# Cross-attention in a decoder block: keys and values of four heads as 11 block products in place of 12

## The chip, the cores and the metric

The kernel runs on one core of a Trainium2 chip. A core has five engines that run their own instruction queues and meet at semaphores: TensorE (PE in the profile, its weight loads PEld), VectorE (DVE), ScalarE (ACT), GpSimd (POOL) and SyncE (SP), whose queue issues the transfers. The metric is the time of one execution on the device in microseconds (us).

## The reference, cut to what matters

A decoder block over x (8 batches of 224 rows of 512) with three sublayers: self-attention with soft-clamped scores, cross-attention to a context (8 batches of 750 rows of 384), and a feed-forward layer with ternary weights. Each is followed by a layer norm of the sum with its input. The change concerns the cross-attention:

```python
q = split_heads(x @ Wq)            # 16 heads of 64
k = split_heads(context @ Wk)      # Wk, Wv: 384 x 1024
v = split_heads(context @ Wv)
sim = jnp.einsum('bhid,bhjd->bhij', q, k) * SCALE
attn = jax.nn.softmax(sim, axis=-1)
out = jnp.einsum('bhij,bhjd->bhid', attn, v)
out = out.transpose(0, 2, 1, 3).reshape(b, sq, HEADS * DIM_HEAD)
return out @ Wo + bo
```

Everything in this sublayer is float32.

## The kernel before

The kernel has three stages, each with an order of work written out by hand (`manual_schedule`): on every engine the instructions stand in the order in which the program writes them, and an engine waits when the next one's operands or buffers are not ready.

Self-attention runs 32 turns (`for m in range(NS)`), each for a pair of heads and two batches. In it GpSimd computes one inverse square root per turn (L129, `nm_i`). Weights lie in a pool of four equal buffers (tag `w`): `wq`, `wk`, `wv`, then `attn_Wo`. When the first three are free, near the end of the stage, `xattn_Wk`, `xattn_Wq` and `xattn_Wv` take their places.

Cross-attention runs over 64 units, one for each batch `b` and pair of heads `hp`, in the loop `for n in range(-1, len(units))`. Turn n does, in TensorE's order:

- `scores` of unit n (L785): six blocks of 125 keys, two heads each. ScalarE copies each block to `cpT` (L793), VectorE takes maxima over the blocks (L795, L799).
- `weighted` of unit n−1 (L879), values times exponentials.
- `keys` of unit n+1 (L748), in two halves of 375 context rows: three products of 128x128 weights with 128x375 context each (384 = 3 x 128). ScalarE copies each half to `ckT` (L755).
- `queries` of unit n+1 (L761). VectorE scales them to `cqT` (L769).
- `half_values` (L736): half the rows of the values for four heads, three row tiles of 125 by 256 columns, three products each; ScalarE copies to `cv` (L743).

Meanwhile VectorE brings the maxima across partitions (`across`: L813 reduces both the maxima and the sums `csm` of the unit before), writes them to `mx_b` (L849) and adds them to the scores (L859), ScalarE exponentiates (L867), and GpSimd adds the exponentials of the six blocks (L869 to L871) into `csm`. `normalise` (L892, L896) scales the weighted sums of unit n−1. The context of a batch lies in one tile `cT`, loaded again for each batch.

Beside this a generator, `weight_steps`, prepares the feed-forward weights, one step per turn: ScalarE sums magnitudes (L643, 12 steps), then rounds (L666) and stores (L676), VectorE clamps (L669). When a batch's last pair is done, `cross_finish` projects its rows (L194) and adds them (L905 on GpSimd, L906).

The pool of PSUM banks (`ps_mm`) has seven that go round: every tile waits for the readers of the one seven before it. A float32 matmul of the program stands in the trace as two records.

Of the kernel before, what the change touches and what calls it, by code (L numbers as in the profile page):

```python
# [10 lines left out]


# [1 line left out]

# [20 lines left out]
SC, CD = 750, 384  # L35
# [11 lines left out]
CT = 125  # L47
NCT = SC // CT
HALF = SC // 2
QH = 4  # L50
NCHUNK = 4
CHUNK = DIM * HID // P // NCHUNK
# [10 lines left out]
def decoder_block(ctx: ExitStack, tc: tile.TileContext, a: dict, out: bass.AP):  # L63
# [47 lines left out]
    wq, wk, wv = ws  # L111
    for i in range(NX // 2, NX):
        load_x(i)
    wo = load_w("attn_Wo", INNER // P, DIM)

    ident = const.tile([P, P], F32, name="ident")
    make_identity(nc, ident)
# [99 lines left out]
    with tc.tile_pool(name="a_sb", bufs=2) as sb, tc.tile_pool(  # L217
# [215 lines left out]
        def self_output(g, i, hp0=0, hp1=NPAIR):  # L433
# [21 lines left out]
            nc.vector.tensor_tensor(x[i], mm, x[i], ALU.add)  # L455
            due.append(i)

        tails, outs, due, scales = {}, {}, [], []

        for i in range(4):  # L460
# [32 lines left out]
        for m in range(NS):  # L493
            g, hp = divmod(m, NPAIR)
            if m > 0:
                self_values(m - 1)
            self_scores(m)
            for i in due:
                scales.append(layernorm([i]))
            due.clear()  # L500
            if m + 1 < NS:
                scale_qk(m + 1)
            if m + 2 < NS:
                project_qk(m + 2)
            sums = inverse_sums(m)
            next(sums)
            if m + 2 < NS:
                head_norms(m + 2)

            c = 1 - hp // 4  # L510
            tiles = opened[g + hp // 4] if g + hp // 4 < NG else ()
            if hp % 4 < len(tiles):
                project_v(tiles[hp % 4], c)
            for _ in sums:
                pass
            for f in scales:
                f()
            scales.clear()
            ahead = opened[g + 1] if g + 1 < NG else ()
            if 2 <= hp < 2 + len(ahead):  # L520
                transpose_xn(ahead[hp - 2])
                copy_xn(ahead[hp - 2])
            if hp in out_at[g]:
                self_output(g - 1, closed[g - 1][out_at[g].index(hp)])
            if hp == 0:
                for i in ahead:
                    square(i)
                if ahead:
                    rms_norms(ahead[0], ahead[-1] + 1)
            if 1 <= hp < 1 + len(ahead):  # L530
                scale_x(ahead[hp - 1])
            if m == NS - 3:
                xwk = load_w("xattn_Wk", KC, INNER)
                xwq = load_w("xattn_Wq", KD, INNER)
                xwv = load_w("xattn_Wv", KC, INNER)

        last = closed[NG - 1]
        for i in last[:2]:
# [12 lines left out]
    wmean = const.tile([P, 3], F32, name="wmean")  # L551
    wscale = const.tile([P, 3], F32, name="wscale")
    parts = const.tile([P, 3, NCHUNK], F32, name="w_parts")
    dram = ctx.enter_context(tc.tile_pool(name="dram", bufs=1, space=bass.MemoryType.DRAM))
    ternary = [dram.tile([P, NCHUNK, CHUNK], BF16, name=f"tern{i}") for i in range(3)]

    wdeq = const.tile([P, 3], F32, name="wdeq")
# [50 lines left out]
    with tc.tile_pool(name="c_sb", bufs=2, reuse_waits="tile") as sb, tc.tile_pool(  # L608
# [1 line left out]
    ) as ps_mm, tc.tile_pool(  # L610
        name="c_ov", bufs=1, space=PSUM, reuse_waits="tile"
    ) as ps_ov, tc.manual_schedule(engines=ENGINES):
        def load_context(b):
            cT = sb.tile([P, KC, SC], F32, name="cT", bufs=1)
            nc.sync.dma_start(
                out=cT, in_=a["ctxT"][b].rearrange("(k p) s -> p k s", p=P)
            )
            return cT

        cT = load_context(0)  # L620
        xwo = load_w("xattn_Wo", INNER // P, DIM)
        bo = sb.tile([P, DIM], F32, name="bo", bufs=1)
        nc.sync.dma_start(out=bo, in_=a["xattn_bo"].partition_broadcast(P))
        stage = sb.tile([P, 2, CHUNK], F32, name="w_stage", bufs=1)
# [64 lines left out]
        def weight_steps():  # L689

            chunks = [(i, c) for i in range(3) for c in range(NCHUNK)]
            stage_chunk(*chunks[0], 0)
            for n, (i, c) in enumerate(chunks):
                yield
                if n + 1 < len(chunks):
                    stage_chunk(*chunks[n + 1], (n + 1) % 2)
                weight_sum(i, c, n % 2)
            yield
            stage_chunk(*chunks[0], 0)
            weight_means()  # L700
            before = None
            for n, (i, c) in enumerate(chunks):
                for h in range(CHUNK // PIECE):
                    yield
                    if before:
                        weight_store(*before)
                    if h == 0 and n + 1 < len(chunks):
                        stage_chunk(*chunks[n + 1], (n + 1) % 2)
                    before = (i, c, n % 2, h)
                    late.append(weight_round(*before))  # L710
            yield
            weight_store(*before)

# [12 lines left out]

        VN = QH * DH

        def values(cT, g, v, half):

            for c0, n in ((3 * half, 2), (3 * half + 2, 1)):
                mm = ps_mm.tile([CT, 2, VN], F32, tag="mm", name="mm_v")
                for i in range(n):
                    c = c0 + i
                    for k in range(KC):
                        nc.tensor.matmul(  # L736
                            mm[:, i, :],
                            lhsT=cT[:, k, c * CT : (c + 1) * CT],
                            rhs=xwv[:, k, g * VN : (g + 1) * VN],
                            start=(k == 0),  # L740
                            stop=(k == KC - 1),
                        )
                nc.scalar.copy(v[:, c0 : c0 + n, :], mm[:, 0:n, :])  # L743

        def keys(cT, hp, kT, c):
            mm = ps_mm.tile([P, HALF], F32, tag="mm", name="mm_k")
            for k in range(KC):
                nc.tensor.matmul(  # L748
                    mm,
                    lhsT=xwk[:, k, hp * P : (hp + 1) * P],  # L750
                    rhs=cT[:, k, c * HALF : (c + 1) * HALF],
                    start=(k == 0),
                    stop=(k == KC - 1),
                )
            nc.scalar.copy(kT[:, c * HALF : (c + 1) * HALF], mm)  # L755

        def queries(xT, hp):
            qT = sb.tile([P, S], F32, name="cqT")
            mm = ps_mm.tile([P, S], F32, tag="mm", name="mm_q")
            for k in range(KD):  # L760
                nc.tensor.matmul(  # L761
                    mm,
                    lhsT=xwq[:, k, hp * P : (hp + 1) * P],
                    rhs=xT[:, k, :],
                    start=(k == 0),
                    stop=(k == KD - 1),
                )

            nc.vector.tensor_scalar(qT, mm, SCALE, None, ALU.mult)  # L769
            return qT  # L770

        def scores(kT, qT):
# [153 lines left out]
        units = [(b, hp) for b in range(B) for hp in range(NPAIR)]  # L926
        steps = weight_steps()
        kq, vs, outs = {}, {}, {}
        late = []

        def half_values(n):

            g = (n + 1) // 2
            if g < len(units) // 2:
                if (n + 1) % 2 == 0:
                    vs[g] = sb.tile([CT, NCT, VN], F32, name="cv")
                values(cT, g % (NPAIR // 2), vs[g], (n + 1) % 2)

        END_U = len(units) - 1
        for n in range(-1, len(units)):  # L940
            if n >= 0:
                b, hp = units[n]
                pT = scores(*kq.pop(n))
                res = across(n == 0, False)
                nm = negated_maxima(res)
                norm = norm_at.get(n)
                if norm is None or norm[0] is not roots:
                    next(steps, None)
            if n >= 1:
                ov = weighted(units[n - 1][1], got, vs[(n - 1) // 2])  # L950
            if n < END_U:
                nb, nhp = units[n + 1]
                if nhp == 0:
                    transpose_x(nb)
                kT = sb.tile([P, SC], F32, name="ckT")
                keys(cT, nhp, kT, 0)
            if n >= 0:
                exponentials(pT, nm)
                got = pT
            if n < END_U:  # L960
                keys(cT, nhp, kT, 1)
                kq[n + 1] = (kT, queries(xT[nb], nhp))
            if n >= 1:
                normalise(*units[n - 1], ov, res)
            if n < END_U:
                half_values(n)
                if nhp == NPAIR - 1 and nb + 1 < B:
                    cT = load_context(nb + 1)
            for f in late:
                f()  # L970
            late.clear()
            if n >= 0 and norm is not None:
                norm[0](*norm[1:])
            if n >= 1 and units[n - 1][1] == NPAIR - 1:

                for i in completes[units[n - 1][0]]:
                    if i != NX - 3:
                        cross_finish(i)
            if n == END_U - 1:
                wg = load_ternary(0, KD, HID)  # L980
                wu = load_ternary(1, KD, HID)
                wd = load_ternary(2, HID // P, DIM)
# [230 lines left out]
```

## Time and profile before

| | |
|---|---|
| Time, median of 3 runs | 1693.07 us (1692.1 to 1693.45) |
| The profiled execution | 1693.18 us, span 1691.4 us |
| TensorE busy, share of the span | 1674.4 us, 99% |
| LDWEIGHTS | 1076.8 us, 64% |
| VectorE | 1247.2 us, 74% |
| ScalarE | 879.1 us, 52% |
| GpSimd | 628.9 us, 37% |
| Keys, L748 | 768 records, 258.5 us busy |
| Values, L736 | 1152 records, 259.1 us busy |
| Granted TensorE clock | 0.999 |

The span is the profiled execution from its first to its last instruction. Busy time of a group is the time in which at least one of its instructions ran: matmuls overlap, so the mean of one (485 ns for keys) is longer than the distance of its start from the next. In the timeline a row has the start, the length and the count of instructions that follow each other; a bracket tells how long the engine was idle before and what ended that. "waits" gives, for an engine's line, the microseconds in all, the times and the longest.

### The profile page before, as it was taken

To read this page: it belongs to the slowest core of one execution; us is meant where nothing else is said; L and a number is where in the kernel's file an instruction comes from. 1 tells how busy PE (TensorE), PEld (TensorE's weight loads), DVE (VectorE), ACT (ScalarE), POOL (GpSimd) and SP (SyncE) were. 2 spreads that over 40 slices of the span, in tenths; PEclk is the share of its full clock that TensorE was granted. 3 is DMA by queue.
4 is the path that set the end of the run, shared out by engine and by line. 5 is a ranking of instruction groups with operands and counts; after the bars stand their busy time and mean duration, and the time that the engine had idled before them with its cause. 6 is when DMAs were issued, how large, how long until landed. Compare 5 with 4: busy or idle time off the path is not lost.

```text
span 1691.4 us, 23310 instructions
## 1 busy us (share of the span) xinstructions
PE 1674.4 (99%) x8602; PEld 1076.8 (64%) x8602; DVE 1247.2 (74%) x2776; ACT 879.1 (52%) x1492; POOL 628.9 (37%) x507
## 2 busy tenths in 40 slices
PE   8999999999999999999999999999999999999998
PEld 4555554555546777776776776776776776774443
DVE  3777776767865776776886886897875776886877
ACT  4655544545523664654664664563453544445663
POOL 3333332333411443443443443443443443443244
PEclk9999999999999999999999999999999999999999
DMA  8000000000133222211221121110000000031333
GB/s 286 1 1 1 1 1 1 1 1 1 38 115 109 76 99 75 75 35 38 69 72 38 54 87 38 36 43 7 1 29 3 4 28 1 1 150 30 71 83 105
DMA packets 61956, 80.47 MB, mean 48 GB/s; under 512 B 36753, under 2 KB 38801, under 8 KB 59409
## 3 DMA queue, kind: packets, MB, share of 16 engines
q1 hardware_dynamic: 61840, 78.97, 14.5%
q8 instruction: 68, 1.11, 0.3%
q14 instruction: 48, 0.39, 0.1%
HBM read 60.34 MB, written 9.96 MB: 42 GB/s over the span
## 4 chain that ended last, share of the span: by engine, by line
PE 97%; DVE 1%; DMA 1%; issue 0%; SPq 0%; POOL 0%; POOLq 0%; DVEq 0%
PE mm_k L748 15%; PE mm_v L736 15%; PE mm_qk L279 12%; PE sc_c L785 9%; PE ov_c L879 9%; PE mm_o L446 6%; PE mm_q L761 6%; PE mm_co L194 6%; PE mm_v L325 6%; PE mm_f L1014 5%; PE sc_a L348 3%; PE ov_a L418 3%; PE dn L1102 2%; DMA cT<-ctxT 1%; PE tr_x L254 0%; PE tr_x L719 0%
## 5 line engine op out<-in xcount | busy, mean ns | idle before, releaser
L869 POOL TENSOR_TENSOR csh<-cpT 125x672 f32<-125x672 f32 x128 | 207.4, 1621 | 577.8 <-DVE cpT L859 552.0
L867 ACT ACTIVATE cpT<-cpT 125x1344 f32<-125x1344 f32 x128 | 169.6, 1325 | 228.9 <-DVE cpT L859 220.1
L748 PE MATMUL mm_k<-cT,xattn_Wk 128*128 128x375 f32 x768 | 258.5, 485 | 1.2 <-DMA cT<-ctxT 1.1
L736 PE MATMUL mm_v<-xattn_Wv,cT 128*125 128x256 f32 x1152 | 259.1, 379 | 0.0
L129 POOL TENSOR_TENSOR nm_i<-nm_q,mhalf 128x28 f32<-128x28 f32 x32 | 153.2, 4786 | 271.1 <-DVE nm_q L306 262.5
L736 PEld LDWEIGHTS mm_v<-xattn_Wv,cT 128*125 128x125 f32 x1152 | 216.3, 188 | 28.9
L793 ACT COPY cpT<-sc_c 125x448 f32<-125x448 f32 x384 | 173.7, 561 | 104.2 <-PE sc_c L785 104.1
L748 PEld LDWEIGHTS mm_k<-cT,xattn_Wk 128*128 128x128 f32 x768 | 140.0, 189 | 101.0 <-issue 12.2
L859 DVE TENSOR_TENSOR cpT<-cpT,mx_b 125x1344 f32<-125x1344 f32 x128 | 193.2, 1550 | 2.2
L795 DVE TENSOR_TENSOR cm<-sc_c,cpT 125x448 f32<-125x448 f32 x128 | 73.9, 619 | 146.5 <-ACT cpT L793 146.5
L785 PE MATMUL sc_c<-cqT,ckT 64*125 64x224 f32 x1536 | 163.1, 358 | 0.0
L879 PE MATMUL ov_c<-cpT,cv 125*64 125x224 f32 x1536 | 159.4, 357 | 0.0
L785 PEld LDWEIGHTS sc_c<-cqT,ckT 64*125 64x125 f32 x1536 | 140.3, 184 | 24.7 <-ACT ckT L755 15.0
L879 PEld LDWEIGHTS ov_c<-cpT,cv 125*64 125x64 f32 x1536 | 104.6, 137 | 47.3 <-issue 18.2
L755 ACT COPY ckT<-mm_k 128x375 f32<-128x375 f32 x128 | 59.2, 462 | 126.1 <-PE mm_k L748 126.1
L358 ACT ACTIVATE pr<-sc_a 128x448 f32<-128x448 f32 (+1 forms) x128 | 61.8, 536 | 91.2 <-PE sc_a L348 91.1
L279 PE MATMUL mm_qk<-xnT,wq 128*128 128x448 f32 (+2 forms) x280 | 107.0, 527 | 1.5 <-DVE xnT L258 1.4
L761 PE MATMUL mm_q<-xT,xattn_Wq 128*128 128x224 f32 x512 | 107.1, 352 | 0.0
L761 PEld LDWEIGHTS mm_q<-xT,xattn_Wq 128*128 128x128 f32 x512 | 96.7, 189 | 16.3
L279 PE MATMUL mm_qk<-xnT,wk 128*128 128x448 f32 x256 | 101.5, 539 | 0.0
L325 PE MATMUL mm_v<-wv,xnT 128*128 128x512 f32 x224 | 100.4, 592 | 0.0
L1014 PE MATMUL mm_f<-ternary,xqT 128*128 128x512 bf16 x448 | 98.7, 379 | 0.9 <-DVE x L906 0.9
(131 smaller groups left out, 2530.2 us busy)
## 6 DMA issues: line engine op xcount, KB each, us to landing
cT<-ctxT SPq DMA_DIRECT2D x8, 1125.0 KB, 5.3
w_stage<-w_gateT SPq DMA_DIRECT2D x8, 1024.0 KB, 4.9
w_stage<-w_upT SPq DMA_DIRECT2D x8, 1024.0 KB, 5.1
w_stage<-w_downT SPq DMA_DIRECT2D x8, 1024.0 KB, 5.2
tern<-w_t SPq DMA_DIRECT2D x24, 256.0 KB, 2.0
ternary<-tern SPq DMA_DIRECT2D x3, 2048.0 KB, 12.4
x<-x SPq DMA_DIRECT2D x14, 256.0 KB, 7.4
out<-x SPq DMA_DIRECT2D x14, 256.0 KB, 2.3
```

Of the source, the lines that this page charges most:

```text
L279: nc.tensor.matmul(mm[:, c0:c1], lhsT=(wq, wk)[w][:, k, hp * P : (hp + 1) * P], rhs=xnT[:, k, g % 2 * G + c0 : g % 2 * G + c1], start=(k = ...
L325: nc.tensor.matmul(mm, lhsT=xnT[:, k, at : at + P], rhs=wv[:, k, c * 512 : (c + 1) * 512], start=(k == 0), stop=(k == KD - 1),)
L736: nc.tensor.matmul(mm[:, i, :], lhsT=cT[:, k, c * CT : (c + 1) * CT], rhs=xwv[:, k, g * VN : (g + 1) * VN], start=(k == 0), stop=(k == KC ...
L748: nc.tensor.matmul(mm, lhsT=xwk[:, k, hp * P : (hp + 1) * P], rhs=cT[:, k, c * HALF : (c + 1) * HALF], start=(k == 0), stop=(k == KC - 1),)
L761: nc.tensor.matmul(mm, lhsT=xwq[:, k, hp * P : (hp + 1) * P], rhs=xT[:, k, :], start=(k == 0), stop=(k == KD - 1),)
L785: nc.tensor.matmul(sc[j][:, i, :], lhsT=kT[h0 : h0 + DH, ct * CT : (ct + 1) * CT], rhs=qT[h0 : h0 + DH, :], start=True, stop=True,)
L793: nc.scalar.copy(pT[:, j, 2 * c2 : 2 * c2 + 2, :], sc[j])
L859: nc.vector.tensor_tensor(pT[:, j], pT[:, j], nm[:CT, j] .rearrange("p (o q) -> p o q", o=1) .to_broadcast([CT, NCT, S]), ALU.add,)
L867: nc.scalar.activation(pT[:, j], pT[:, j], AF.Exp)
L869: nc.gpsimd.tensor_tensor(half, pT[:, j, 0:3], pT[:, j, 3:6], ALU.add)
L879: nc.tensor.matmul(ov[h0 : h0 + DH, :], lhsT=v[:, ct, hq * DH : (hq + 1) * DH], rhs=pT[:, j, ct, :], start=(ct == 0), stop=(ct == NCT - 1),)
L1014: nc.tensor.matmul(mm, lhsT=xqTs[i][:, k, :], rhs=w[:, k, cols], start=(k == 0), stop=(k == KD - 1),)
```

## The change

Take the context of a batch as 2 x 3 blocks A11 … A23 (two halves of 375 rows, three parts of 128 of the inner dimension) and the weights of four heads as 3 x 2 blocks B11 … B32 (128 columns each). The product has four blocks C11 … C22, each a sum of three block products: 12. The kernel after uses a bilinear scheme that needs 11, four of which have sums of blocks as operands:

- GpSimd builds the weight sums once, in the turns 0, 1, 3 and 4 of self-attention (`room_sums`), in a weight buffer that `attn_Wo` takes later (`load_wo`), and they go to DRAM (`sums_w`). Four context sums per batch are built during the batch before (`sum_context`).
- `half_products` runs the products of one operand, keys or values, for four heads. Three PSUM tiles x_, z_ and w_ accumulate; x_ is copied several times on the way, since it holds partial sums that several blocks share. ScalarE makes six copies, GpSimd adds two results (C11, C22), VectorE one (C21).
- Turns with odd n make the keys of the next two units, turns with even n the values of both units (`turn_products`); before, each turn made the keys of one and half the values. Seven products come before the queries, four after. `ckT` and `cv` have one buffer each.
- A key product streams 375 columns as before; a value product is three matmuls of 128 columns, where before one had 256.
- `xattn_Wk` and `xattn_Wv` are no longer held whole: each set of blocks is loaded at the end of a turn for the turn after next (`load_blocks`, three transfers), into `xw`.
- There are two context tiles, one for even and one for odd batches, each loaded a batch ahead.
- The queries' scaling goes from VectorE to ScalarE. Weight sums and rounds on ScalarE come after the first seven products (`acts`). No weight step is made in turns with hp = 6, in which `transpose_x` of the next batch now stands. `cross_finish` is called once per turn at most (`spare`).

```diff
+    def room_sums(j):
+        blk = room[:, : KC * INNER].rearrange("p (k g c n) -> p k c g n", k=KC, c=2, n=P)
...
+        sub = lambda y, p, q: nc.gpsimd.tensor_tensor(y, p, q, ALU.subtract)
+        sub(o1, b(0, 1), b(0, 0))
+        yield
+        sub(b(0, 1), b(1, 1), b(0, 1))
...
+            nc.sync.dma_start(out=sums_w[:, j, :, i, :], in_=y)
...
+        def load_blocks(j, g):
+            src = a[("xattn_Wk", "xattn_Wv")[j]].rearrange("(k p) n -> p k n", p=P)
+            c = 2 * g * P
+            nc.sync.dma_start(out=xw[:, j, 0:KC], in_=src[:, :, c : c + P])
+            nc.sync.dma_start(
+                out=xw[:, j, KC : KC + 2], in_=src[:, 1:KC, c + P : c + 2 * P]
+            )
+            nc.sync.dma_start(out=xw[:, j, KC + 2 :], in_=sums_w[:, j, g])
...
+            for _ in range({0: 2, 1: 3, 3: 2, 4: 3}.get(m, 0)):
+                next(room_steps[m // 3])
+            if m == 1:
+                room_load(1)
+            if m == 4:
+                load_wo()
...
-                weight_sum(i, c, n % 2)
+                acts.append(partial(weight_sum, i, c, n % 2))
...
-        def values(cT, g, v, half):
-        def keys(cT, hp, kT, c):
+        def half_products(b, j, product, dest):
...
+            x_, z_, w_ = acc
+            product(x_, a11, b11, True)
+            nc.scalar.copy(m1, x_)
+            product(z_, a12, b21, True)
+            product(z_, a13, b31, False)
+            nc.scalar.copy(c11, z_)
+            product(x_, s2, t2, False)
+            nc.scalar.copy(u2, x_)
+            product(w_, s3, t3, True)
+            product(w_, a23, b32, False)
+            nc.scalar.copy(c22, w_)
+            product(x_, s1, t1, False)
+            nc.scalar.copy(u4, x_)
+            nc.gpsimd.tensor_tensor(c11, c11, m1, ALU.add)
+            nc.gpsimd.tensor_tensor(c22, c22, u4, ALU.add)
+            yield
+            product(w_, a22, t4n, False)
+            product(w_, a23, dif, False)
+            nc.vector.tensor_tensor(c21, w_, u2, ALU.add)
+            product(x_, s4, b22, False)
+            product(x_, a13, b32, False)
+            nc.scalar.copy(c12, x_)
+            yield
...
+        def key_product(mm, c, w, start):
+            nc.tensor.matmul(
+                mm, lhsT=w, rhs=c, start=start, stop=True, skip_group_check=True
+            )
+
+        def value_product(mm, c, w, start):
+            for t in range(NCT // 2):
+                nc.tensor.matmul(
+                    mm[:, t, :], lhsT=c[:, t * CT : (t + 1) * CT], rhs=w,
+                    start=start and t == 0, stop=True, skip_group_check=True,
+                )
...
-            nc.vector.tensor_scalar(qT, mm, SCALE, None, ALU.mult)
+            nc.scalar.activation(qT, mm, AF.Identity, scale=SCALE)
...
-                pT = scores(*kq.pop(n))
+                pT = scores(kq.pop(n), qTs.pop(n))
...
+            products = turn_products(n)
+            next(products, None)
+            for f in acts:
+                f()
...
+                qTs[n + 1] = queries(xT[nb], nhp)
             if n >= 0:
                 exponentials(pT, nm)
...
+                if hp == NPAIR - 2 and b + 1 < B:
+                    transpose_x(b + 1)
+            for _ in products:
+                pass
             if n >= 1:
                 normalise(*units[n - 1], ov, res)
...
+                    load_blocks((n + 1) % 2, d % (NPAIR // 2))
+            if n >= 0:
+                if hp == NPAIR - 2 and b + 2 < B:
+                    load_context(b + 2)
+                if 2 <= hp < 6 and b + 1 < B:
+                    sum_context(b + 1, hp - 2)
...
+            if spare:
+                cross_finish(spare.pop(0))
```

## The prediction

> **What bounds the kernel now.** I read the page's busy table first, then the waits of TensorE, then the timeline of one turn engine by engine. The busy table and the waits of TensorE (who waited for whom, total us, times, longest):
>
> ```profile
> PE 1674.4 (99%) x8602; PEld 1076.8 (64%) x8602; DVE 1247.2 (74%) x2776; ACT 879.1 (52%) x1492; POOL 628.9 (37%) x507
> ...
> PE mm_k L748 <- DMA cT<-ctxT: 1.1, 2, 0.9
> ```
>
> TensorE never rests; in cross-attention it waits only 1.1 us, for a context transfer. A busy PE alone proves little, so the timeline of one turn (start us, length us, instructions) has to show that the instructions stand end to end:
>
> ```profile
> 613.30 2.54 PE L785 MATMUL sc_c<-cqT,ckT 64*125 64x224 f32 x24
> 615.76 2.49 PE L879 MATMUL ov_c<-cpT,cv 125*64 125x224 f32 x24
> 618.19 4.05 PE L748 MATMUL mm_k<-cT,xattn_Wk 128*128 128x375 f32 x12
> 622.08 1.67 PE L761 MATMUL mm_q<-xT,xattn_Wq 128*128 128x224 f32 x8
> 623.59 4.05 PE L736 MATMUL mm_v<-xattn_Wv,cT 128*125 128x256 f32 x18
> 627.56 2.54 PE L785 MATMUL sc_c<-cqT,ckT 64*125 64x224 f32 x24
> ```
>
> By differences of starts: scores 2.46, weighted sums 2.43, keys 3.89, queries 1.51, values 3.97; a turn is 14.26 us without a gap. [...] Within the runs the key records start 0.315 us apart (once 0.42, where the shape changes from the weighted sums), the value records 0.216. So every record removed shortens the turn, until another engine's loop is longer. Those engines in the same turn (ScalarE, VectorE, GpSimd):
>
> ```profile
> 614.41 2.71 ACT L793 COPY cpT<-sc_c 125x448 f32<-125x448 f32 x6 [0.48 <-PE sc_c L785]
> 616.95 1.97 ACT L643 ACTIVATE w_stage<-w_stage 128x2048 f32<-128x2048 f32 x1
> ...
> 620.38 0.47 ACT L755 COPY ckT<-mm_k 128x375 f32<-128x375 f32 x1 [1.37 <-PE mm_k L748]
> 624.29 2.79 ACT L867 ACTIVATE cpT<-cpT 125x1344 f32<-125x1344 f32 x2 [3.44 <-DVE cpT L859]
> ```
>
> ```profile
> 619.32 0.60 DVE L813 TRANSPOSE_TENSOR_REDUCE mx_r<-csm 128x14 f32<-128x448 f32 x1
> ...
> 622.64 3.02 DVE L859 TENSOR_TENSOR cpT<-cpT,mx_b 125x1344 f32<-125x1344 f32 x2
> 625.57 0.38 DVE L769 TENSOR_SCALAR cqT<-mm_q 128x224 f32<-128x224 f32 x1
> ```
>
> ```profile
> 625.75 1.62 POOL L869 TENSOR_TENSOR csh<-cpT 125x672 f32<-125x672 f32 x1 [7.97 <-DVE cpT L859]
> 627.45 0.66 POOL L870 TENSOR_TENSOR csm<-csh 125x224 f32<-125x224 f32 x1
> ...
> 631.37 0.67 POOL L871 TENSOR_TENSOR csm<-csm,csh 125x224 f32<-125x224 f32 x1
> ```
>
> There is a loop through these: VectorE reduces csm (619.32), adds the maxima (622.64), ScalarE exponentiates (624.29), GpSimd sums from 625.75 to 632.04, and the next reduction, at 619.32 + 14.26 = 633.58, needs that. The loop itself takes 632.04 − 619.32 = 12.72 us: 1.5 us of slack now.
>
> [...] eight records with 128 columns loaded and 128 streamed, from the timeline of the start:
>
> ```profile
> 14.26 1.06 PE L279 MATMUL mm_qk<-xnT,wq 128*128 128x128 f32 x8
> ```
>
> One of them lasts 0.275 (mean by shape in that window), so they start (1.06 − 0.275) / 7 = 0.112 us apart: loads do hide. [...] L870 takes 0.66 mostly, but 0.99 in the 24 turns in which it meets VectorE's rounding L669.
>
> **The change part by part.**
>
> *Keys* (removed): 12 products per batch and four heads become 11, so 24 records become 22: 2 × 0.315 = 0.63 us, in 8 × 4 = 32 groups: **−20.2**.
>
> *Values*: 36 records of 256 columns, 36 × 0.216 = 7.77 us, become 11 products × 3 tiles × 2 = 66 records of 128 columns. Price of one: 0.109 at least (the transposes L254 start so far apart[...]), 0.112 by the row above. If loads did not hide it would be the 0.188 of the LDWEIGHTS row. I take 0.110[...]: 7.26 us, 0.51 less, × 32: **−16.4** (−12 at 0.112, −18.5 at 0.109).
>
> *Context*: two alternating context tiles, loaded nine turns ahead: the 1.1 us goes: **−1.1**.
>
> *Products in one turn*: keys of two pairs in odd turns, values of both in even ones. A keys turn is 2.46 + 2.43 + 7.1 + 1.51 = 13.5 us, a values turn 13.7. Shape changes per turn stay as many. Counting from a turn's start (t = 0), the products begin at 4.9; seven end near 9.4, queries near 10.9, the last four at 13.5.
>
> *Accumulators*: x_ is copied and then accumulated further, so TensorE now waits for ScalarE. The first copy of x_ can start at 5.8 and ends at 6.25; its next product comes at 6.9. Each later copy has two products (1.26 us) before its bank is written: slack about 0.6 us. Queued behind such a wait is all of TensorE. Bounds: 0 if ScalarE is free (sc_c copies end at 3.8), 0.5 us a turn if not. I take 0.
>
> *ScalarE*: six copies per turn, 0.35 apart back to back (L755 626.98 to L743 627.33), for two key and two value copies, and the query scaling: some +1.3 us. In turns with weight preparation its work is 2.7 + 2.8 + 2.6 + 0.4 + 2.5 = 11 of 13.6. It moves: the weight sum (2.2) now stands after the seventh product's copy, 10.0 to 12.2; the query scaling and the first exponential follow at 12.5 instead of 11.0. Late next: the second exponential (15.0), the last copy c12 (15.4, or 1.9 into the next turn), the first sc_c copy by 0.8. VectorE's adds start at 10.1 then, still ahead of ScalarE, so this doesn't grow. c12 is for the later pair; the scores at t = 13.5 need c11 and c21.
>
> *VectorE*: c21 = one add of 375 columns, about 0.5, behind the maxima adds (end 12.3): ready at 12.8, scores at 13.5. The query scaling (0.38) leaves. Free of charge, hidden behind the last two products; without that cover 0.5 a keys turn, 16 in all.
>
> *GpSimd*: two adds of 375 columns per turn. Between the rows of 224 (0.66) and 512 columns (L905, 1.27): 1.0 each. c11 can run at 7.6, c22 at 10.1 to 11.1, before the exponential sums at 12.5. Context sums, 4 per batch, follow the sums. Busy 6.3 + 2.0 + 0.5 of 13.6: free.
>
> *Self-attention*: ten weight sums of 128x512 on GpSimd, 1.27 each, two or three per turn after nm_i (4.8 of a 13 us turn), and ten stores of them. The room tile's load takes the place of attn_Wo's, issued at 26.6, landed by 37; the first sum comes near 57. attn_Wo is needed from the ninth turn, near 158. Free; uncovered 12.7.
>
> *Transfers*: three loads per block set, 0.13 to 0.33 MB (0.25 MB takes 2.0 us), issued more than a turn before use, behind weight staging on SP's queue. Free. The ternary loads now wait for the last value product: up to 4 us later, but they landed 15 us before the first mm_f. One output projection per turn is the same work. [...]
>
> Sum: −20.2 − 16.4 − 1.1 + 1 = −36.7. The profiled execution took 1693.18 with a span of 1691.4, 0.1 above the median of 1693.07. So the span becomes 1654.7 and the time **1657** (1656.4 rounded up for waits at the edges).
>
> **Rivals.**
>
> *Half the gain is given back by ScalarE* (faster, less so). For: its work is moved into the dense end of the turn, and the scores' second pair reuses a bank that c12 must free. Against: by the above, the lateness is bounded by 0.8. Price: 0.5 us in the 37 turns with weight work, 18 us: 1675.
>
> *Short records don't hide their loads* (the change doesn't do what it says). Values break even at 7.77 / 66 = 0.118 and the whole change at (7.77 + 0.63) / 66 = 0.127 us. At 0.120 it is 1657 + 2112 × 0.010 = 1678. Against: the eight records at 0.112.
>
> *GpSimd's loop becomes the bound* (slower). If c11 and c22 come to stand in the loop, because late copies put them between exponential and sums[...], the loop is 12.72 + 2.0 = 14.7 us: 64 × 0.45 = +29: 1722. It decides from 1.54 us in the loop (14.26 − 12.72). For: GpSimd's slack shrinks to 0.9. Against: the copies come 1.4 us before the exponential ends.
>
> **How the numbers follow.** Forecast (1650 to 1665) 0.73; half the gain 0.13; loads not hidden 0.05, a fifth of it slower; GpSimd's loop 0.06, all but a little slower; anything else 0.03. 0.2% is 3.4 us, about what a measurement can tell from no change. Faster 0.91, same 0.02, slower 0.07. The range 1650 to 1678 takes in the lower bound of the value records (−2), fewer edges, and the half gain.
>
> **What would show it.** 704 key records 0.315 and 2112 value records 0.110 apart; turns of 13.5 and 13.7; no PE wait for DMA cT. Wrong if TensorE shows waits for the copies of x_ or for c21, a GpSimd busy without pause, or value records over 0.118 apart.

## The result, and the profile after

The changed kernel takes 1665.58 us (median of 4, 1665.15 to 1666.01) against 1693.12 for the kernel before on the same chip (1692.1 to 1693.45): ratio 0.9838, 95% interval 0.9821 to 0.9855, 27.5 us faster. The forecast was 1657: the sign holds and so does the wide range (1650 to 1678), but the time lies 0.6 us above the narrow one (1650 to 1665), and the point is 8.6 us too low.

The busy table and the head of the chain that ended last, from the page of after (engine, busy us, share, instructions; the chain's shares of the span):

```profile
span 1663.4 us, 26236 instructions
PE 1644.7 (99%) x9498; PEld 1086.4 (65%) x9498; DVE 1304.3 (78%) x2776; ACT 965.8 (58%) x1684; POOL 812.0 (49%) x677
...
PE 87%; DVE 8%; issue 2%; ACT 2%; POOL 0%; DMA 0%; POOLq 0%; SPq 0%; ACTq 0%; DVEq 0%
```

TensorE is still 99% busy, but the chain is not TensorE's alone any more: 8% of it runs through VectorE. The busy share couldn't have told this. The waits of TensorE in cross-attention (who waited for whom, total us, times, longest), from after:

```profile
PE sc_c L918 <- DVE cpT L992: 3.1, 6, 1.3
PE sc_c L918 <- DVE ckT L866: 0.4, 1, 0.4
```

The wait for the context transfer is gone. A new one has come: the scores wait for VectorE's adds of the negated maxima (L992). The listed 3.1 us are only a part of it. The timeline of TensorE shows a turn of keys and one of values without trouble, then two turns with it (start us, length us, instructions, the idle time ahead of them):

```profile
567.84 2.54 PE L918 MATMUL sc_c<-cqT,ckT 64*125 64x224 f32 x24
570.30 2.49 PE L1012 MATMUL ov_c<-cpT,cv 125*64 125x224 f32 x24
...
581.37 2.54 PE L918 MATMUL sc_c<-cqT,ckT 64*125 64x224 f32 x24
...
608.71 1.40 PE L918 MATMUL sc_c<-cqT,ckT 64*125 64x224 f32 x10
610.57 1.86 PE L918 MATMUL sc_c<-cqT,ckT 64*125 64x224 f32 x14 [0.46 <-DVE cpT L992]
...
624.57 4.18 PE L918 MATMUL sc_c<-cqT,ckT 64*125 64x224 f32 x24
628.68 2.49 PE L1012 MATMUL ov_c<-cpT,cv 125*64 125x224 f32 x24
```

In the first turns the scores take 570.30 − 567.84 = 2.46 us, as before, and the turn of keys 581.37 − 567.84 = 13.53. At 608.71 the scores take 3.65, at 624.57 they take 4.11 (to the weighted sums at 628.68): their records stand apart, which the view shows as a longer group and mostly not as a wait. I took for each of the 64 turns the time from the first score record to the next other matmul, less 2.46, and added up what was over: 14.3 us in after, 1.2 before. Ten turns carry it (number 0 of cross-attention, and 6, 7, 15, 38, 39, 44 to 47). Turn 0's 0.64 is of another kind, the wait for the c21 add (L866) in the list above. This excess is the whole of the missing time: the streaming did what was forecast, and more (below).

What makes those turns late shows in VectorE's timeline of two earlier ones, number 2 (from 554.03) and number 5 (from 595.18), and in GpSimd's of the same times. L946 reduces the maxima and csm, L953 and L975 are the small copies that carry the maxima across partitions, L992 adds them to the scores; L861 is GpSimd's c11 add, L862 its c22 add, L1004 the last of its sums of exponentials:

```profile
560.99 0.60 DVE L946 TRANSPOSE_TENSOR_REDUCE mx_r<-csm 128x14 f32<-128x448 f32 x1
561.63 1.55 DVE L953 COPY mx_s<-mx_r 32x28 f32<-32x28 f32 x4
563.21 0.20 DVE L958 TENSOR_REDUCE mx_n<-mx_s 32x14 f32<-32x56 f32 x1
...
565.08 3.02 DVE L992 TENSOR_TENSOR cpT<-cpT,mx_b 125x1344 f32<-125x1344 f32 x2
...
602.52 0.60 DVE L946 TRANSPOSE_TENSOR_REDUCE mx_r<-csm 128x14 f32<-128x448 f32 x1
603.16 1.59 DVE L953 COPY mx_s<-mx_r 32x28 f32<-32x28 f32 x4
...
605.40 1.37 DVE L975 COPY mx_n<-mx_n 32x21 f32<-32x21 f32 x3
...
607.49 1.55 DVE L992 TENSOR_TENSOR cpT<-cpT,mx_b 125x1344 f32<-125x1344 f32 x1
```

```profile
559.99 0.92 POOL L1004 TENSOR_TENSOR csm<-csm,csh 125x224 f32<-125x224 f32 x1
561.75 1.00 POOL L861 TENSOR_TENSOR cv<-cv,cm 125x384 f32<-125x384 f32 x1 [0.84 <-ACT cv L853]
564.42 1.01 POOL L862 TENSOR_TENSOR cv<-cv,cu 125x384 f32<-125x384 f32 x1 [1.68 <-ACT cu L860]
...
603.34 0.97 POOL L861 TENSOR_TENSOR ckT<-ckT,cm 128x375 f32<-128x375 f32 x1
605.39 0.98 POOL L862 TENSOR_TENSOR ckT<-ckT,cu 128x375 f32<-128x375 f32 x1 [1.08 <-ACT cu L860]
```

In turn 2 the four small copies L953 take 1.55 us together, where the same four took 0.77 before. Singly, in the trace, they are 0.18, 0.96, 0.18 and 0.18 us: the second starts at 561.82, when GpSimd's c11 add (561.75 to 562.74) has just begun, and ends 0.04 us after that add's end. From the reduction of csm to the adds is then 565.08 − 560.99 = 4.09 us, against 3.32 before. The loop from csm's reduction to the next one is 13.85 us here (VectorE 4.09, first exponential 1.64, GpSimd's first sum 1.47, the rest of its sums 6.57, 0.08), a little longer than the mean of a keys and a values turn, 13.67, so the lateness grows. In turn 5 it has brought the second group of copies, L975, under the c22 add as well: 1.37 us for three that take 0.53. VectorE's stretch is 607.49 − 602.52 = 4.97, the loop (from 602.52 to the next reduction, 617.25) 14.73, and turn 6 is the first in which the scores wait for L992: their next bank is the one that L992 still reads.

The groups of small instructions by shape (count, busy us, mean ns, idle before), first of before, then of after; L820 and L842 became L953 and L975:

```profile
L820 DVE COPY mx_s<-mx_r 32x28 f32<-32x28 f32 x252 | 45.8, 182 | 4.8
L842 DVE COPY mx_n<-mx_n 32x21 f32<-32x21 f32 x189 | 31.9, 169 | 3.8
```

```profile
L953 DVE COPY mx_s<-mx_r 32x28 f32<-32x28 f32 x252 | 65.6, 260 | 4.8
L975 DVE COPY mx_n<-mx_n 32x21 f32<-32x21 f32 x189 | 49.8, 264 | 3.9
L958 DVE TENSOR_REDUCE mx_n<-mx_s 32x14 f32<-32x56 f32 x64 | 12.8, 200 | 2.2
```

### The profile page after: what moved, and what is told of

Its sections match the earlier page's. It is cut to its first block, busy times and chain, and to the rows that moved or that the text cites. A ratio compares the mean times of both kernels' runs of the same rounds, so it can differ in the third digit from the quotient of the medians.

```text
span 1663.4 us, 26236 instructions
## 1 busy us (share of the span) xinstructions
PE 1644.7 (99%) x9498; PEld 1086.4 (65%) x9498; DVE 1304.3 (78%) x2776; ACT 965.8 (58%) x1684; POOL 812.0 (49%) x677
## 4 chain that ended last, share of the span: by engine, by line
PE 87%; DVE 8%; issue 2%; ACT 2%; POOL 0%; DMA 0%; POOLq 0%; SPq 0%; ACTq 0%; DVEq 0%
PE mm_qk L324 12%; PE sc_c L918 8%; PE ov_c L1012 8%; PE mm_o L491 6%; PE mm_co L239 6%; PE mm_v L370 6%; PE mm_f L1173 6%; PE k_x L879 5%; PE v_x L885 5%; PE mm_q L894 5%; PE k_w L879 4%; PE v_w L885 4%; PE sc_a L393 3%; PE ov_a L463 3%; PE dn L1261 2%; PE k_z L879 2%
## 5 line engine op out<-in xcount | busy, mean ns | idle before, releaser
L992 DVE TENSOR_TENSOR cpT<-cpT,mx_b 125x1344 f32<-125x1344 f32 x128 | 193.2, 1551 | 2.2
L918 PE MATMUL sc_c<-cqT,ckT 64*125 64x224 f32 x1536 | 172.0, 360 | 4.2 <-DVE cpT L992 3.1
L1004 POOL TENSOR_TENSOR csm<-csm,csh 125x224 f32<-125x224 f32 x128 | 97.9, 765 | 10.0
L491 PE MATMUL mm_o<-w_room,oT 128*128 128x512 f32 (+1 forms) x224 | 98.8, 594 | 0.0
L239 PE MATMUL mm_co<-xattn_Wo,coT 128*128 128x512 f32 (+1 forms) x256 | 98.6, 594 | 0.0
L1003 POOL TENSOR_TENSOR csm<-csh 125x224 f32<-125x224 f32 x128 | 93.6, 731 | 10.0
L380 ACT COPY v<-mm_v 32x512 f32<-32x512 f32 (+2 forms) x80 | 46.3, 579 | 64.1 <-PE mm_v L370 63.5
```

Of the source, the lines that this page charges most:

```text
L239: nc.tensor.matmul(mm[row : row + m, :], lhsT=oT[:, k, at : at + m], rhs=w[:, k, :], start=(k == 0), stop=(k == NPAIR - 1),)
L491: nc.tensor.matmul(mm[row : row + lhsT.shape[-1], :], lhsT=lhsT, rhs=wo[:, hp, :], start=(hp == 0), stop=(hp == NPAIR - 1),)
L918: nc.tensor.matmul(sc[j][:, i, :], lhsT=kT[h0 : h0 + DH, ct * CT : (ct + 1) * CT], rhs=qT[h0 : h0 + DH, :], start=True, stop=True,)
L992: nc.vector.tensor_tensor(pT[:, j], pT[:, j], nm[:CT, j] .rearrange("p (o q) -> p o q", o=1) .to_broadcast([CT, NCT, S]), ALU.add,)
```

## The experiments

Two theories stood against each other. Theory G: GpSimd's c11 add runs beside VectorE's small copies and holds them up, the loop gets longer than the turn, and the scores wait. Theory A: ScalarE, with its added copies and the weight work moved behind them, is late, and VectorE with it.

**The two adds in the other order**

```
-            nc.gpsimd.tensor_tensor(c11, c11, m1, ALU.add)
             nc.gpsimd.tensor_tensor(c22, c22, u4, ALU.add)
+            nc.gpsimd.tensor_tensor(c11, c11, m1, ALU.add)
```

> The kernel after with GpSimd's two adds of a turn in the other order: c22 first, c11 behind it; everything else is as it was. After has lost 14.3 us in scores that wait for the bank of the negated maxima, in ten of the 48 turns. Theory G (GpSimd's c11 add runs beside VectorE's small copies of the maxima, one of which then takes 0.96 us where it took 0.18, so the loop from one turn's sums of exponentials to the next is 13.8 us where a turn has 13.67): c11 moves behind those copies, they come back to about 0.2 us, the first copy of the scores by ScalarE is no longer later from turn to turn, and 11 us of the 14.3 come back: 1654, at most 1658. Theory A (ScalarE's added copies and the weight work moved behind them make ScalarE late, and VectorE with it): the order of two GpSimd adds is nothing to ScalarE, so 1665, within 1.5. If c22 takes c11's place at the copies (it waits for the last of ScalarE's copies of its half, about 0.5 us later), the stall moves from one copy to the next and theory G would also give 1662 to 1666; the durations of the copies tell these apart.

Measured: 1652.14 us (1651.35 to 1652.69; before 1693.37 on this chip), ratio 0.9758 (0.9744 to 0.9771). All 13 us are back, from the order of two adds; the time is 2 us under the 1654 that theory G gave. (The expectation speaks of 48 turns; cross-attention has 64.) VectorE's and GpSimd's timelines of the same turn in this kernel, where L861 is now the c22 add and L862 the c11 add:

```profile
559.84 0.60 DVE L946 TRANSPOSE_TENSOR_REDUCE mx_r<-csm 128x14 f32<-128x448 f32 x1
560.47 0.77 DVE L953 COPY mx_s<-mx_r 32x28 f32<-32x28 f32 x4
...
563.15 3.02 DVE L992 TENSOR_TENSOR cpT<-cpT,mx_b 125x1344 f32<-125x1344 f32 x2
```

```profile
563.55 1.00 POOL L861 TENSOR_TENSOR cv<-cv,cu 125x384 f32<-125x384 f32 x1 [3.79 <-ACT cu L860]
564.52 1.00 POOL L862 TENSOR_TENSOR cv<-cv,cm 125x384 f32<-125x384 f32 x1
```

Both adds now lie beside VectorE's adds of the maxima, which take 3.02 us all the same; the copies take 0.77, and VectorE's stretch is 3.31. The scores' excess falls to 1.3 us, and the chain on its page is TensorE's again:

```profile
PE 98%; DVE 1%; DMA 0%; issue 0%; POOL 0%; SPq 0%; POOLq 0%; ACT 0%; DVEq 0%; ACTq 0%
```

How late the turns are shows in ScalarE's first copy of scores, in us after the turn's first score record (1.11 when nothing is late; from the traces):

| Turn | 1 | 2 | 3 | 4 | 5 | 6 |
|---|---|---|---|---|---|---|
| before | 1.96 | 1.11 | 1.11 | 1.11 | 1.11 | 1.11 |
| after | 1.71 | 1.92 | 1.94 | 2.16 | 2.43 | 3.48 |
| other order of adds | 1.70 | 1.36 | 1.33 | 1.36 | 1.33 | 1.36 |

**The same work, with more of GpSimd's**

```
-            nc.gpsimd.tensor_tensor(c11, c11, m1, ALU.add)
+            nc.gpsimd.tensor_tensor(m1, c11, m1, ALU.add)
             nc.gpsimd.tensor_tensor(c22, c22, u4, ALU.add)
+            nc.gpsimd.tensor_copy(c11, m1)
```

> The kernel after with the c11 add writing to the first summand's buffer, and a GpSimd copy of 375 columns to c11 behind the c22 add: the add keeps its place and its inputs, GpSimd has one instruction of about 0.5 to 0.8 us more in a turn, behind c22. Theory G: what counts is whether something of GpSimd's lies beside VectorE's small copies, not how much GpSimd does in all; the added copy lies under VectorE's adds of the negated maxima, so 1665, within 2[...]. Theory A: 1665 too. A third theory L (GpSimd is itself the loop's bound, by its busy time of a turn): 0.5 to 0.8 us more in each of 48 turns, with the loop at 13.8 already over the turn: 1690 to 1700.

Measured: 1665.07 us (1661.61 to 1666.15), within 0.5 of after, with 28 us more of GpSimd's busy time (840.2 against 812.0). Had these 28 us lengthened the loop, as theory L says, the time would be near 1665.6 + 28 = 1694. So GpSimd's load is not what binds (theory L is out). Where its add lies is.

**Without the two adds**

```
-            nc.gpsimd.tensor_tensor(c11, c11, m1, ALU.add)
-            nc.gpsimd.tensor_tensor(c22, c22, u4, ALU.add)
```

> The kernel after without GpSimd's two adds in cross-attention, so that two of the four blocks of keys and of values lack one of their two summands; nothing else is left out. Theory G: no GpSimd work beside VectorE's copies, none behind it either: the scores' excess falls from 14.3 us to about 2, 1653, from 1650 to 1656. Theory A: ScalarE's copies and the weight work stand where they stood, 1665, within 2. The difference to the run with the two adds in the other order is what the adds cost where they lie under VectorE's other work: under theory G 0 to 3 us.

Measured: 1651.22 us (1650.97 to 1651.7). This version leaves out summands that the result needs; it shows only what the adds cost. It lies 0.9 us below the other order: there the adds cost next to nothing, under VectorE's longer work. Nearly all of the 0.9 is one copy that the other order still leaves held, for 0.99 us in turn 43; turn 44 loses 0.78 there and nothing here. Theory A is out as the main cause, since all of ScalarE's work is still in place here.

**The weight work at the top again**

```
-                acts.append(partial(weight_sum, i, c, n % 2))
+                weight_sum(i, c, n % 2)
...
-                    acts.append(lambda at=before: late.append(weight_round(*at)))
+                    late.append(weight_round(*before))
```

> The kernel after with ScalarE's weight sums and weight roundings issued at the top of their turn's slot again, as in the kernel before; GpSimd's adds as in after. Theory A: the weight work is out of the way of the copies between the halves, and of the exponentials: 10 to 12 us come back, 1654 to 1656. Theory G: the copies of the maxima still meet the c11 add, and the scores still wait: 1663 to 1667; ScalarE's part of it (its weight sum ahead of the first exponential in the first turns) is worth at most 3.

Measured: 1662.61 us (1661.92 to 1663.06), 3.0 less than after, just under what theory G gave (1663 to 1667). Turns 10 to 14 are on time here (first copy at 1.11 in each, where after drifts from 1.42 to 2.27), and the first exponential, which no longer stands behind the weight sum, starts at 11.4 to 11.55 of these turns instead of 12.4 to 14.0. Turns 7, 38, 39 and 44 to 47 still lose, and the scores' excess is 9.4 us instead of 14.3. ScalarE has a part in about 3 of the 13 us lost; the size is rough, since the four runs of the kernel with more of GpSimd's work alone lie 4.5 us apart.

**The copies in another form of instruction**

The order of adds is after's; VectorE's copies become maxima over an axis of one element.

```
-                nc.vector.tensor_copy(
-                    side[:, kinds, :, g], quarter[g * Q32 : (g + 1) * Q32, kinds]
-                )
+                nc.vector.tensor_reduce(
+                    side[:, kinds, :, g],
+                    quarter[g * Q32 : (g + 1) * Q32, kinds].rearrange(
+                        "p k (b o) -> p k b o", o=1
+                    ),
+                    AX.X, ALU.max,
+                )
...
-                nc.vector.tensor_copy(
-                    res[g * Q32 : (g + 1) * Q32, own, :, 0], res[:Q32, own, :, 0]
-                )
+                nc.vector.tensor_reduce(
+                    res[g * Q32 : (g + 1) * Q32, own, :, 0], res[:Q32, own], AX.X, ALU.max
+                )
```

> The kernel after with GpSimd's adds in its own order (c11 first), and VectorE's seven small copies of a turn (four that bring the quarters to one partition range, three that spread the results) written as maxima over an axis of one element, which give the same values. Theory F (GpSimd's add holds up the copy's form of instruction alone: in after a reduction of 32x56 beside the same add takes 0.200 us, as anywhere, where a copy takes up to 0.96): the seven take about 0.2 us each wherever the add lies, nothing grows late, 1652 to 1655. Theory H (every small VectorE instruction from SBUF to SBUF is held up, and the reductions just happened to lie better): 1663 to 1667, with some of the seven at 0.5 to 1.0 us.

Measured: 1651.91 us (1651.47 to 1652.42; before 1692.64), ratio 0.9758 (0.9744 to 0.9772). The groups by shape, and turn 2 on VectorE and on GpSimd:

```profile
L953 DVE TENSOR_REDUCE mx_s<-mx_r 32x28 f32<-32x28 f32 x252 | 48.6, 193 | 4.7
L979 DVE TENSOR_REDUCE mx_n<-mx_n 32x21 f32<-32x21 f32 x189 | 31.5, 167 | 3.8
```

```profile
561.30 0.82 DVE L953 TENSOR_REDUCE mx_s<-mx_r 32x28 f32<-32x28 f32 x4
```

```profile
561.64 1.00 POOL L861 TENSOR_TENSOR cv<-cv,cm 125x384 f32<-125x384 f32 x1 [1.05 <-ACT cv L853]
```

The c11 add runs from 561.64 in the middle of the four, and they take 0.82 us; none of the 455 in this run takes more than 0.20. Same data, same places, same add beside them: it was the copy's form that was held up. This is the second, independent cure, with the adds where after has them, and it decides against theory H.

**The c11 add in two halves**

```
-            nc.gpsimd.tensor_tensor(c11, c11, m1, ALU.add)
+            w = (HALF + 1) // 2 if j == 0 else P // 2
+            for at in (slice(0, w), slice(w, None)):
+                nc.gpsimd.tensor_tensor(c11[..., at], c11[..., at], m1[..., at], ALU.add)
```

> The kernel after with the c11 add as two adds, one for each half of its columns, one behind the other in the same place. If a VectorE copy waits for the end of the GpSimd instruction that runs (theory E), no copy is held for longer than one half, 0.5 to 0.6 us, and a second copy can be held by the second half only if GpSimd starts it first: the longest copy falls from 0.96 to about 0.55 us, and half to all of the 13 us that the other order of the adds brought come back, 1653 to 1659. If a copy and an add share the memory for as long as both run (theory F2), the work is the same and so is the loss: 1664 to 1668, the two halves costing GpSimd some 0.1 us more.

Measured: 1664.45 us (1662.21 to 1665.9): no gain. The time is the one that was said for theory F2, so theory E's number fails; its mechanism holds, because the held copies end with the half beside them. In turn 2 the trace has copies of 0.58 and 0.53 us, each ending just after one half (halves from 561.815 to 562.409 and 562.367 to 562.955; copies end at 562.453 and 562.999): the second half starts before the first copy is through and catches the next copy. The timelines of GpSimd and of VectorE:

```profile
561.82 1.14 POOL L863 TENSOR_TENSOR cv<-cv,cm 125x192 f32<-125x192 f32 x2 [0.66 <-ACT cv L853]
```

```profile
561.87 1.52 DVE L955 COPY mx_s<-mx_r 32x28 f32<-32x28 f32 x4
```

These are the copies over 0.28 us in the traces of these runs (of 455 each):

| Kernel | held | their time over 0.18, us | time, us |
|---|---|---|---|
| before | 0 | 0 | 1693.12 |
| after | 69 | 36.4 | 1665.58 |
| other order | 1 | 0.8 | 1652.14 |
| more of GpSimd's | 73 | 41.0 | 1665.07 |
| without adds | 0 | 0 | 1651.22 |
| weight work at top | 68 | 34.4 | 1662.61 |
| maxima for copies | 0 | 0 | 1651.91 |
| two halves | 104 | 37.1 | 1664.45 |

All 69 of after lie beside the c11 or the c22 add, and every one ends 26 to 47 ns behind the add's end. A copy was held until the add was over; it wasn't merely slowed. Which of the two began first decided it: every copy of after that began 12 ns or more into one of the two adds (71, the latest 816 ns into it) ended 26 to 47 ns after its end, and none of the 42 that began before the add, or within 6 ns of its start, was held by it. The bound of 0.28 leaves out short holds beside the context sums, up to 0.27 us. Of 36 us of holding 13 reach the end: the rest is slack, as in the turns from 17 to 34, which stay on time with one copy held for 0.1 to 0.5 us.

**Values by the plain products**

```
-            return half_products(
-                units[n][0], 1, value_product,
...
+            return plain_values(units[n][0], v)
...
+                    for k in range(KC):
+                        nc.tensor.matmul(
+                            mm[:, i, :], lhsT=ctx_[:, k, r, t * CT : (t + 1) * CT],
+                            rhs=w[:, k, :], start=(k == 0), stop=(k == KC - 1),
+                        )
+                nc.scalar.copy(v[:, c0 : c0 + 2, :], mm)
```

> Keys by 11 block products, values by 12: the values' turns go back to the plain products (256 columns a product, three copies by ScalarE, no sums by GpSimd or VectorE), with the order of the two adds c22 first, c11 second in the keys' turns. The weight sums for the values are still made beforehand, and not used. It stands against the kernel with the other order of adds in both kinds of turn, 1652.1. By my price for the values (2112 records at 0.110 us for 1152 at 0.216): 16.5 us more, 1668.6; by the spacing that the trace of after shows (0.109): 18.6 us more, 1670.7. If short records had hidden less than that, or if the sums of the values' turns cost time in that kernel too, the difference is under 14: below 1666.

Measured: 1670.54 us (1670.16 to 1670.95), ratio 0.9869 (0.9855 to 0.9883). Against the other order's 1652.14 that is 18.4 us, and 18.8 by the ratios to before (0.0111 of 1693): the values' half of the change is worth what the spacing of records says, 18.6 (worked out below), and their sums cost nothing visible.

**Both cures of order together**

This is the kernel after with the edits of the first and the fourth experiment.

> Both together: the two adds in the other order (1652.1 alone) and ScalarE's weight work at the top of its turn's slot (1662.6 alone, 3 less than after). Under theory G the weight work costs only what it adds to a lateness that the held copies start; with the copies free there is nothing left to win but the last 1.3 us of the scores' excess: 1651 to 1653. If ScalarE's part were a loss of its own, the 3 us would add up: 1649.

Measured: 1651.26 us (1650.78 to 1652.86), ratio 0.9757 (0.9743 to 0.977). That is not 3 but 0.9 us below the other order alone, within both runs' spread; in its trace no copy is held and the scores' excess is 0.5 us. So the weight work costs at most 1 us of its own once the copies are free. This kernel, that with the other order and that with maxima for copies beat both the kernel before (by 2.4%) and the changed one (by 0.8%); among the three the runs don't choose.

## Why the prediction was right or wrong

*Keys, −20.2*: right. 704 records, their starts 0.315 us apart (the median, in the trace of after).

*Values, −16.4*: a size slightly off. 2112 records start 0.109 us apart, not 0.110 (an estimate between the 0.109 and the 0.112 that the prediction had from the trace of before): (36 × 0.216 − 66 × 0.109) × 32 = 18.6, confirmed by the run with plain values. The loads hide, as the argument from the eight mm_qk records said; the rival of short records that don't hide them (from 0.118) is out. In the trace of after each of these loads lasts 0.188 us, and they begin 0.109 apart, so that each overlaps the next.

*Context, −1.1*: right, no wait for it is left. *The +1 of the sum*: the author's estimate, with no measured figure behind it; nothing of it is seen. With the other order TensorE's busy time is 1635.5, so 1674.4 − 1635.5 = 38.9 us less, against 20.2 + 18.6 = 38.8 for keys and values alone; its idle time, span less busy time, falls from 17.0 to 14.6.

*Turns of 13.5 and 13.7*: 13.53 and 13.80 where nothing is late. *Accumulators, 0*: right, after shows no wait of a block product for ScalarE. *VectorE's c21 add*: 0.54 to 0.55 us, hidden but for a single wait of 0.4. *Self-attention's weight sums*: 1.47 us each rather than 1.27, and hidden: the first scores of cross-attention start at 528.48, at 529.50 before.

*ScalarE, "this doesn't grow"*: right by itself. With the copies free, the first exponential starts at 12.1 to 12.35 of a turn (12.5 was said), the first copy of scores is 0.22 to 0.25 late in turns 2 to 6, and the lateness doesn't grow. In after it made the loss some 3 us larger, by adding to a lateness that the held copies met; this coupling of two things costed at nothing each was not in the prediction. The rival that gave ScalarE half the gain (1675) had the wrong engine.

*GpSimd, "c11 can run at 7.6 … free"*: **this step failed.** The add's length (1.0) and place (7.7 to 8.7 of turn 2) were right. It was free only by GpSimd's own busy time. Beside it lay VectorE's small copies, at 6.7 to 7.4 and 8.1 to 8.6 of a turn in the trace of before, inside the loop whose slack the same prediction had put at 0.9 us. The held copies take 0.77 of that in turn 2, and GpSimd's last sums 0.28 (L1004 0.92 us instead of 0.66 beside VectorE's two-input maximum L932, which took 0.75 instead of 0.63). So the term "12.72" of the loop came out as 13.85 in turn 2, and as 14.73 when the c22 add met the copies too. The third rival named the right loop, but the wrong way in: the adds never stood in GpSimd's part of it. Its price was a loop of 14.7 in every turn; the true one came to that only now and then (the likeness of 14.73 is chance), and cost 13 us and not 66.

The trace of before held a warning, and the prediction quotes it: GpSimd's L870 takes 0.99 us instead of 0.66 in the 24 turns in which it meets VectorE's rounding L669. I didn't ask whether GpSimd's add could hold VectorE's seven copies of 0.17 to 0.18 us. In after it did: the 71 that began 12 ns or more into one of the two adds were held to its end (26 to 47 ns behind it), the 42 that began before it or within 6 ns of its start were not. The maxima over one element that took the copies' place took 0.167 to 0.193 us in the mean, with the adds where after has them. In after, 37 reciprocals of 32x14 lay beside the two adds, each at 0.227 to 0.229 us, as alone.

The sum for the version without the fault (the other order of adds): its span is 1650.1 where 1654.7 was forecast, lower by 2.2 for the values, 1 for that estimate of +1, and 1.4 that I didn't size; cross-attention starts 1.3 earlier in it than before (528.24 against 529.50). So the forecast's nearness is partly luck: the held copies cost 13.4 us (1665.58 − 1652.14), and terms that were too careful by some 5 (1657 − 1652.14) hid a third of it. The wide range held the result because it made room for ScalarE's half gain, which isn't what happened.

## What to carry to other kernels

Before an added instruction on VectorE or GpSimd is called free because its engine has room, lay it in time against the other of the two, down to copies of 0.2 us, and look in a trace for which of them take longer beside it: here a copy of 0.18 us took up to 0.98. A hold inside a loop has to be set against the loop's slack (0.9 us here), not against the engine's idle time. Where it falls badly, a small edit may do: here the order of two independent adds was enough (1652.14 us instead of 1665.58), and so was another form of the copy (1651.91). A busy share of 99% hid 14.3 us of such stalls here: compare the length of the same group of matmuls from turn to turn.

## What the runs showed of the hardware

In after, a VectorE copy of 32x28 float32 values, 0.18 us by itself, took up to 0.98 us beside a GpSimd add of 1.0, and one of 32x21 up to 1.01 for 0.17. All 71 copies that began 12 ns or more behind an add's start were held to its end, and none of the 42 that began before it or within 6 ns of its start was held by it. Maxima of the same sizes (0.19 and 0.17 us in the run with maxima for copies) and reciprocals of 32x14 (0.23) took no longer beside an add. Cutting the add in two didn't let a second copy through: 104 copies were held instead of 69, for the same total (37.1 and 36.4 us). VectorE's adds of 1344 columns from SBUF and PSUM took 1.55 us with and without a GpSimd add beside them. And the lateness grew for five turns in which TensorE lost nothing (scores at 2.47 us in turns 1 to 5), before the next two lost 1.2 and 1.65: a short window of the trace could have shown no loss.
